# Layer 0 feed-forward: first products over 256 tokens per weight tile, first weights streamed through a ring

## The chip, the core and the metric

The kernel runs on one core of a Trainium2 chip. The time of a run is the device time of one execution in microseconds. The engines are named as the profile names them: PE (TensorE, matmuls; PEld its weight loads), DVE (VectorE), ACT (ScalarE), POOL (GpSimd) and SP (SyncE, which issues most DMAs; its queue is SPq). All data are fp32 unless a row says otherwise.

## What is computed

2048 tokens of 512 features pass two layers, each a cross-attention over a context and a feed-forward (FFN), with a layer norm before each attention and FFN and a residual add behind it. The change touches layer 0's FFN:

```python
inter = xf @ c1_w.T @ c2_w.T                       # rank 16, 1792 columns
blk = inter.reshape(B * T, 56, 32)                 # 56 blocks of 32
idx = jnp.argmax(blk, axis=-1) + jnp.arange(0, 1792, 32)
h = jax.nn.relu(jnp.einsum('bkm,bm->bk', w1[idx], xf))
out = jnp.einsum('bk,bkm->bm', h, w2t[idx])
```

For every token, one of 32 hidden units is chosen in each of 56 blocks. The kernel computes all 1792 hidden values as dense products, keeps the chosen ones (others become zero), and multiplies by the second weights.

## The kernel before

The 2048 tokens are 16 tiles of 128. Layer 0's attention goes over eight pairs of tiles (i = 0 to 7), and behind it comes the FFN, again pair by pair (p = 0 to 7). The instructions of each engine stand in an order that a scheduler of the program's framework makes when the program is built, from priorities and estimated costs. On the chip each engine works its list off in that order and waits for others by semaphores. SP issues its DMAs in order too, with at most eight under way, each waiting for the one eight before it.

A product of matrices is done in Winograd's form of Strassen's scheme: 7 products of quarter matrices in place of 8, in the order `ORDER` = 1, 5, 6, 2, 7, 3, 4 (`winograd`). It needs four sums of quarters of each factor (`four_sums`, L127, on POOL). `keep` copies a partial result on ACT, `put` finishes a quarter of the output.

- **First weights (W1).** During the attention, W1's four quarters are loaded (L610) and their four sums made on POOL. All seven stay in SBUF as tiles of 128 x 2 x 896.
- **Second weights (W2).** They are loaded in pieces during the attention (L516), summed on POOL, stored to HBM (L522), and loaded at the FFN's start (L687, seven loads of 0.9 MB).
- **Preparing a pair.** Layer norm (L104 to L115), transposes on PE (L181) and copies on ACT (L220) give the transposed tokens `xT`. `pz` (L227) and `pzs` (L236) give the rank-16 values, and `key_product` (L279) multiplies them by c2 into `pi`. `first_largest` finds the largest of each block: DVE reduce (L267), DVE compare (L268), a POOL multiply called `e` (L272), DVE reduce (L273). `keep_choice` turns the result on PE (`ptc`, L285), casts it on ACT (L287) and stores it to HBM (L288). `spread_choice` (L673) reads it back onto all partitions, eight DMAs for each part of the hidden columns.
- **Front (first products).** The hidden columns are seven blocks of 128, in two parts, `PARTS` = ((0, 3), (3, 4)). For each part and each of the 7 products, matmuls (L727) of 128 columns, half a pair's tokens. `keep` is L735 (ACT), `put` is L742 (DVE add), L744 (DVE: keeps the value where the spread choice `ch` names this unit, else zero) and L747 (ACT relu). The output is `gT`.
- **Back (second products).** Matmuls (L770) of 256 columns over `gT`, its sums `gs` (POOL), and W2; DVE adds (L778) the result to the tokens `X`.

The loop over pairs puts the back of the pair before between the two parts of a front. The preparation and choice of the next pair are placed there too:

```python
front(xq, gq, ch.pop((p, 0)), 0)
...
back(p - 1, last, between if choosing else lambda i: None)
...
front(xq, gq, ch.pop((p, 1)), 1)
if more:
    ch[p + 1, 1] = spread_choice(p + 1, 1)
    xq = sums(xT)
last = gq + out_sums(gq)
```

Pairs 0 and 1 are prepared and chosen during the attention. The first products accumulate in PSUM tiles `ph`; `pi` is a PSUM tile of four banks of its own. Layer 1 follows, with its products at L901, its weights loaded by SP as tiles of 256 KB.

Of the kernel before, what the change touches and what calls it, by code (L numbers as in the profile page):

```python
# [16 lines left out]
P = 128  # L17
# [3 lines left out]
C = D // P  # L21
# [14 lines left out]
def tile_kernel(  # L36
# [147 lines left out]
    with ExitStack() as l0:  # L184
# [15 lines left out]
        W1 = [w1pool.tile([P, 2, 2 * QW], F32, name=f"w1_{k}", tag=f"w1_{k}") for k in range(4)]  # L200
        w1s = [w1pool.tile([P, 2, 2 * QW], F32, name=f"w1s_{k}", tag=f"w1s_{k}") for k in range(3)]
        W1 += [w1s[0], w1s[1], W1[UNUSED[False]], w1s[2]]


        prepool = l0.enter_context(tc.tile_pool(name="ffnprep", bufs=2, reuse_waits="tile"))
        W2S = [dram.tile([P, HC, 256], F32, name=f"w2s_{k}", tag=f"w2s_{k}") for k in range(4)]

        def prep_steps(p, ps_t):

            xT = prepool.tile([P, C, 2 * P], F32, name=f"xT2_{p}", tag="xT2")  # L210
# [22 lines left out]
            def summed():  # L233
                z = prepool.tile([P, 2 * P], F32, name="z", tag="z", bufs=1)
                pz = ps_t.tile([P, 2 * P], F32, name="pzs", tag="pt")
                nc.tensor.matmul(pz, SUM4.rearrange("p q r -> p (q r)"), held["z"], start=True, stop=True)  # L236
                nc.scalar.copy(z, pz)
                return xT, z
# [5 lines left out]
        def prep(p, ps_t):  # L244
            for step in prep_steps(p, ps_t):
                made = step()
            return made

        def sums(xT):
            q = [xT[:, 2 * k : 2 * k + 2, m * P : (m + 1) * P] for k in range(2) for m in range(2)]  # L250
            s = [prepool.tile([P, 2, P], F32, name=f"xs{k}", tag=f"xs{k}") for k in range(3)]
# [5 lines left out]
        CHOICE = [dram.tile([4 * NBQ, 2 * P], BF16, name=f"choice_{p}", tag=f"choice_{p}") for p in range(NT // 2)]  # L257
# [23 lines left out]
        def keep_choice(p, choices, ps_t):  # L281
# [6 lines left out]
            nc.sync.dma_start(CHOICE[p], ct)  # L288

        def new_choices():  # L290
            return [prepool.tile([P, 4 * NBQ], F32, name="choice", tag="choice", bufs=2) for _ in range(2)]

        with ExitStack() as pa:
# [234 lines left out]
            steps = [prep_steps(p, ps_t) for p in range(2)]  # L528
# [11 lines left out]
            def two_quarters(p, v):  # L540
# [3 lines left out]
                for q in (2 * v, 2 * v + 1):  # L544
                    pi = ps_m.tile([P, 1, D], F32, name="pi0", tag="pm")[:, :, 0:QW]

                    with tc.high_priority(offset=100) if two else ExitStack():
                        key_product(pi[:, 0], made[p][1], q // 4, q % 4)
# [32 lines left out]
            NP = NT // 2  # L581
# [9 lines left out]
            for i in range(NP):  # L591
# [5 lines left out]
                with tc.issue_after(due) if i + 2 < NP else ExitStack():  # L597
                    if store is not None:
                        store()
                    if i:  # L600
# [5 lines left out]
                if 1 <= i < 5:  # L606
                    cols_v = slice(QW * ((i - 1) // 2), QW * ((i - 1) // 2) + QW)
                    for k in (2, 3) if i % 2 else (0, 1):
                        h = 2 * QW * (k // 2)
                        nc.sync.dma_start(  # L610
                            W1[k][:, :, cols_v],
                            w1[:, 2 * (k % 2) : 2 * (k % 2) + 2, h + cols_v.start : h + cols_v.stop],
                        )
# [8 lines left out]
                if i:  # L622
# [5 lines left out]
                    with started_behind(normed):  # L628
                        sum_up()
                        for n in range(*{3: (0, 2), 4: (2, 4), 5: (4, 6), 6: (6, 7), 7: (7, 8)}.get(i, (0, 0))):  # L630
                            w = [t[:, :, QW * (n // 4) : QW * (n // 4) + QW] for t in W1]
                            four_sums(nc.gpsimd, w[4:], *w[:4], False, (n % 4,))
# [17 lines left out]
            xq = sums(made[0][0])  # L650
            xT, choices = made[1][0], choices[1]

        PARTS = ((0, 3), (3, HC - 3))
        with ExitStack() as pb:
            wk = pb.enter_context(tc.tile_pool(name="ffnwork", bufs=2, reuse_waits="tile"))
# [8 lines left out]
            def spread_choice(p, u):  # L666

                c0, n = PARTS[u]
                t = wk.tile([P, 2, n, 2 * P], BF16, name=f"ch{u}_{p}", tag=f"ch{u}", bufs=1)
                d = CHOICE[p].rearrange("(i j b) t -> b i j t", i=2, b=4)  # L670
                for b in range(4):
                    for i in range(2):
                        nc.sync.dma_start(  # L673
                            t[32 * b : 32 * b + 32, i],
                            d[b : b + 1, i, c0 : c0 + n].to_broadcast([32, n, 2 * P]),
# [3 lines left out]
            ch = {(p, u): spread_choice(p, u) for p, u in ((0, 0), (0, 1))}  # L679
# [5 lines left out]
            for i in ORDER:  # L685
# [31 lines left out]
            def front(xq, gq, ch, u):  # L717
# [3 lines left out]
                def bank():  # L721
                    return ps_p.tile([P, n, P], F32, name="ph", tag="pp")

                def mm(i, ps, first):
                    for c in range(n):
                        for d in range(2):
                            nc.tensor.matmul(  # L727
                                ps[:, c, :], W1[LEFT[i]][:, d, (c0 + c) * P : (c0 + c + 1) * P],
                                xq[RIGHT[i]][:, d, :],
                                start=first and c == 0 and d == 0, stop=d == 1, skip_group_check=True,  # L730
                            )

                def keep(k, ps):
                    h = wk.tile([P, n, P], F32, name=f"hk{k}", tag="hk", bufs=3)
# [3 lines left out]
                def put(i, m, ps, kept):  # L738
                    if (i, m) == (1, 1):
                        ps = keep(3, ps)  # L740
                    if kept is not None:
# [3 lines left out]
                        g, ch[:, i, :, m * P : (m + 1) * P], downcol, ps, ALU.is_equal, ALU.mult  # L745
# [3 lines left out]
                winograd(bank, mm, keep, put)  # L749

            def out_sums(gq):
# [5 lines left out]
                for u in range(2):  # L757
                    four_sums(nc.gpsimd, [t[u] for t in s], *(t[u] for t in gq), False)
                return s

            def back(p, gq, between):


                def chunk(q, c):
                    u = int(c >= PARTS[1][0])
                    return q[u][:, c - PARTS[u][0], :]

                def mm(i, ps, first):
# [5 lines left out]
                    between(i)  # L774
# [13 lines left out]
            last = None  # L788
            for p in range(NP):
# [713 lines left out]
```

## Time and profile before

| what | value |
|---|---|
| median of 3 runs | 1797.55 us (1796.15 to 1797.73) |
| the profiled execution, its own time | 1799.84 us |
| its span in the profile | 1798.1 us |
| mean granted TensorE clock | 0.999 |
| layer 0's attention | 0 to 180.65 us of the span |
| layer 0's FFN | 180.65 to about 556 us |

The page gives busy time of each engine, the DMA queues, the chain of work that ended last, and groups of instructions. L numbers are lines of the kernel before. A table by windows gives for each stretch its length, the busy time of PE, PEld, DVE, ACT and POOL with the number of records, the granted clock, the DMA share and GB/s. A line of the chain gives start, length and work; a line of a timeline also gives, in brackets, the idle time before it and what released it.

### The profile page before, as it was taken

What the parts mean: (1) busy time and instruction counts of PE and PEld (TensorE: products, weight loads), DVE (VectorE), ACT (ScalarE), POOL (GpSimd) and SP (SyncE); (2) the same over time, 40 slices, a digit from 0 to 9 for tenths busy, and PEclk for the clock granted to TensorE, in tenths of its full rate; (3) what the DMA queues carried; (4) which work ended last, traced back from release to release, by engine and by line L of the source; (5) the groups of instructions that cost most, each with busy time, mean ns of one, the idle gap of its engine ahead of it and who ended that gap; (6) DMA issues with size and microseconds to landing.
All of it is one profiled execution on the core that took longest, in us unless ns stands there. A gap on an engine that the chain in (4) does not pass through costs nothing.

```text
span 1798.1 us, 29543 instructions
## 1 busy us (share of the span) xinstructions
PE 1773.8 (99%) x11364; PEld 1446.9 (80%) x11364; DVE 968.0 (54%) x1733; ACT 623.0 (35%) x1157; POOL 715.4 (40%) x622
## 2 busy tenths in 40 slices
PE   8999999999999999999999999999999999999999
PEld 4544988988998788888888888888888888888864
DVE  5887565555524454455455444555554555555557
ACT  4654322222112423334234333442343433433311
POOL 1552433443327766764324234332243332322320
PEclk9999999999999999999999999999999999999999
DMA  9632400000014344454444454444445444443513
GB/s 248 195 108 66 166 23 22 22 22 21 13 55 148 130 158 152 141 194 153 147 147 130 143 162 126 132 147 136 135 131 163 137 129 143 149 146 117 182 48 94
DMA packets 169500, 219.31 MB, mean 122 GB/s; under 512 B 19024, under 2 KB 108112, under 8 KB 168720
## 3 DMA queue, kind: packets, MB, share of 16 engines
q1 hardware_dynamic: 155712, 206.91, 37.1%
q10 hardware_dynamic: 13648, 10.50, 2.0%
q8 instruction: 91, 1.49, 0.4%
q14 instruction: 49, 0.40, 0.1%
HBM read 176.74 MB, written 32.21 MB: 116 GB/s over the span
## 4 chain that ended last, share of the span: by engine, by line
PE 88%; POOL 4%; DMA 3%; DVE 2%; ACT 1%; issue 1%; SPq 0%; POOLq 0%; ACTq 0%; DVEq 0%
PE b L901 49%; PE ph L727 10%; PE po L770 10%; PE pv L1130 3%; PE sc L1070 3%; PE pd L1350 3%; PE pq L397 3%; POOL so L127 2%; PE pk L374 2%; PE pr L1048 1%; PE pt L181 1%; PE pi L279 1%; POOL prob L1077 1%; DMA x<-in_x 1%; DMA wos<-wo 1%; PE ptk L1033 1%
## 5 line engine op out<-in xcount | busy, mean ns | idle before, releaser
L1161 DVE TENSOR_TENSOR x<-x,b 128x512 f32<-128x512 f32 x224 | 153.9, 687 | 228.7 <-PE b L901 228.7
L127 POOL TENSOR_TENSOR so<-oT 128x512 f32<-128x512 f32 x64 | 80.1, 1273 | 485.0 <-ACT oT L1137 485.0
L901 PE MATMUL b<-tx,wq 128*128 128x256 f32 x1024 | 237.8, 380 | 3.2 <-DVE qT L994 1.7
L901 PE MATMUL b<-wo,so 128*128 128x256 f32 x1024 | 231.7, 379 | 1.8 <-issue 1.8
L901 PEld LDWEIGHTS b<-tx,wq 128*128 128x128 f32 x1024 | 193.9, 190 | 31.9 <-POOL tx L127 2.5
L901 PEld LDWEIGHTS b<-wo,so 128*128 128x128 f32 x1024 | 194.5, 190 | 28.6 <-issue 2.2
L901 PE MATMUL b<-xt,wq 128*128 128x256 f32 x768 | 183.5, 381 | 0.9 <-DVE kv L965 0.9
L901 PE MATMUL b<-wo,oT 128*128 128x256 f32 x768 | 181.5, 379 | 0.0
L901 PEld LDWEIGHTS b<-xt,wq 128*128 128x128 f32 x768 | 144.4, 190 | 21.2 <-DVE kv L965 1.3
L901 PEld LDWEIGHTS b<-wo,oT 128*128 128x128 f32 x768 | 144.8, 190 | 19.9 <-issue 1.0
L909 ACT COPY keep<-b 128x512 f32<-128x512 f32 x144 | 83.8, 583 | 181.7 <-PE b L901 178.8
L1137 ACT COPY oT<-pv 128x512 f32<-128x512 f32 x64 | 37.4, 584 | 280.6 <-PE pv L1130 270.8
L994 DVE TENSOR_TENSOR qT<-b,keep 128x512 f32<-128x512 f32 x96 | 66.1, 689 | 116.9 <-PE b L901 114.5
L901 PE MATMUL b<-wkv,sc 128*128 128x256 f32 x512 | 117.0, 380 | 0.0
L1082 DVE TENSOR_REDUCE mx<-prob 128x8 f32<-128x512 f32 x64 | 43.9, 686 | 125.0 <-POOL prob L1077 125.0
L901 PEld LDWEIGHTS b<-wkv,sc 128*128 128x128 f32 x512 | 96.6, 190 | 13.8 <-issue 1.0
L272 POOL TENSOR_TENSOR e<-e,down 128x896 f32<-128x896 f32 (+1 forms) x40 | 68.0, 1706 | 93.9 <-DVE e L268 89.8
L997 ACT ACTIVATE qsq<-qT 128x512 f32<-128x512 f32 x128 | 80.3, 627 | 70.5 <-DVE qT L994 58.6
L770 PE MATMUL po<-w,gT 128*128 128x256 f32 x448 | 101.9, 382 | 0.0
L1094 POOL TENSOR_TENSOR prob<-prob,mx 128x512 f32<-128x512 f32 x64 | 66.5, 1060 | 86.0 <-DVE mx L1093 83.6
L770 PEld LDWEIGHTS po<-w,gT 128*128 128x128 f32 x448 | 84.0, 190 | 18.7 <-issue 7.8
L901 PE MATMUL b<-wkv,ct 128*128 128x256 f32 x384 | 93.0, 384 | 2.6 <-DVE mx L1093 2.0
(211 smaller groups left out, 3053.0 us busy)
## 6 DMA issues: line engine op xcount, KB each, us to landing
wq<-in_wq SPq DMA_DIRECT2D x104, 256.0 KB
wo<-in_wo SPq DMA_DIRECT2D x104, 256.0 KB
wq<-wqs SPq DMA_DIRECT2D x96, 256.0 KB
wo<-wos SPq DMA_DIRECT2D x96, 256.0 KB
wkv<-in_wkv SPq DMA_DIRECT2D x52, 256.0 KB
wkv<-wks SPq DMA_DIRECT2D x48, 256.0 KB
wqs<-wq SPq DMA_DIRECT2D x32, 256.0 KB
aT<-tb ACTq DMA_DIRECT2D x256, 32.0 KB
```

What stands on the lines that cost most here:

```text
L127: ins = eng.tensor_tensor(s[k], *pairs[k], op)
L272: nc.gpsimd.tensor_tensor(e3, e3, down[:, None, :].to_broadcast([P, k, BLK]), ALU.mult)
L397: nc.tensor.matmul(pq, xT[:, tt, c, :], WQ[:, c, :], start=c == 0, stop=c == C - 1)
L727: nc.tensor.matmul(ps[:, c, :], W1[LEFT[i]][:, d, (c0 + c) * P : (c0 + c + 1) * P], xq[RIGHT[i]][:, d, :], start=first and c == 0 and d == ...
L770: nc.tensor.matmul(ps, chunk(gq[LEFT[i]], c), W2[RIGHT[i]][:, c, :], start=first and c == 0, stop=c == HC - 1, skip_group_check=True,)
L901: last = nc.tensor.matmul(out[:, h, :], lhs(h, c), rhs(h, c), start=first and h == 0 and c == 0, stop=c == 1, skip_group_check=True,)
L909: keeps.append(nc.scalar.copy(e, ps).ins)
L994: ins = nc.vector.tensor_add(o, ps, kept.rearrange("p j (b t) -> p j b t", t=S))
L997: nc.scalar.activation(qsq[:, 4 * th : 4 * th + 4, 2 * hh : 2 * hh + 2, :], o, AF.Square)
L1070: score = nc.tensor.matmul(sc[b * S : (b + 1) * S, 4 * a + j, :], qT[:, at, j, :], kT[:, bb * S : (bb + 1) * S], start=True, stop=True,)
L1094: ins = nc.gpsimd.tensor_tensor(pr, pr, mx[:, 1, :, None].to_broadcast([P, 8, S]), ALU.mult)
L1161: added.append(nc.vector.tensor_add(xq[:, i, j], xq[:, i, j], ps).ins)
```

## The change

- `PARTS` has four parts, ((0, 2), (2, 2), (4, 2), (6, 1)). A front works on a quad, four tiles (512 tokens), with matmuls of 256 columns. There are four quads (`NQ`).
- W1 is no longer kept in SBUF. Its sums are made in pieces during the attention (`piece_of_w1`, loaded at i = 2 to 5, summed one turn later, stored to HBM four turns after the load), and each front product takes its weight tile from a ring of eight tiles (`load_ring`: 128 x 2 x 256, 256 KB, or half of it for the last part). A tile is loaded when the product that used its slot has been issued; the first eight are loaded at i = 7. Over the kernel 112 tiles are loaded.
- The choice of both pairs of a quad goes to one HBM tensor, and `spread_choice` reads 512 tokens, in four parts of eight DMAs: 128 DMAs in all as before. The second pair's choice is stored at the FFN's start.
- W2's loads are spread over the fronts of the first quad, two with each of its first parts.
- The token sums `xs` are made once for a quad, 128 x 512 each, and the output sums `gs` for each pair in four parts.
- A quad's first back follows the last part of its front; its second back follows the first part of the next quad's front.
- Preparation and choices of the next quad are placed by three tables (FIRST for the first quad, PLAN and LATE for the others).
- The first quad's first part uses the `pi` banks, as one tile of four banks, in place of `ph` tiles.
- The pools of FFN work tiles and of prepared tokens lie on the right side of SBUF; only the pool of `gT` and `gs` stays on the left.

```diff
@@ -197,17 +197,41 @@
             nc.gpsimd.tensor_copy(SUM4[:, q], SUM4[:, 0])
+        PARTS = ((0, 2), (2, 2), (4, 2), (6, 1))
+        NP = NT // 2
+        NQ = NT // 4
+        W1S = [
+            [dram.tile([P, 2, n * P], F32, name=f"w1s_{k}_{u}", tag=f"w1s_{k}_{u}") for u, (_, n) in enumerate(PARTS)]
+            for k in range(4)
+        ]
         W2S = [dram.tile([P, HC, 256], F32, name=f"w2s_{k}", tag=f"w2s_{k}") for k in range(4)]
+        RING = 8
+        ring, rung = [], []
+        W1_ORDER = [(u, i) for _ in range(NQ) for u in range(len(PARTS)) for i in ORDER]
+        def load_ring():
+            if len(ring) == len(W1_ORDER):
+                return
+            u, i = W1_ORDER[len(ring)]
+            (c0, n), k = PARTS[u], LEFT[i]
+            w = w1pool.tile([P, 2, n * P], F32, name=f"w1r_{len(ring)}", tag="w1r", bufs=RING)
+            at = QW * 2 * (k // 2) + c0 * P
+            nc.sync.dma_start(
+                w, w1[:, 2 * (k % 2) : 2 * (k % 2) + 2, at : at + n * P] if k < 4 else W1S[k - 4][u]
+            )
+            ring.append(w)
+        prepool = l0.enter_context(tc.tile_pool(name="ffnprep", bufs=2, side="right", reuse_waits="tile"))
+        def new_tokens(q):
+            return prepool.tile([P, C, 4 * P], F32, name=f"xT2_{q}", tag="xT2")
+        def prep_steps(p, ps_t, quad):
+            xT = quad[:, :, 2 * P * (p % 2) : 2 * P * (p % 2) + 2 * P]
             held = {}
             def norm_tile(m):
...
@@ -525,7 +544,27 @@
-            steps = [prep_steps(p, ps_t) for p in range(2)]
+            def piece_of_w1(u):
+                c0, n = PARTS[u]
+                w = [
+                    w1pool.tile([P, 2, n * P], F32, name=f"w1p_{u}_{k}", tag="w1r", bufs=RING) for k in range(4)
+                ]
+                for k in range(4):
+                    at = 2 * QW * (k // 2) + c0 * P
+                    nc.sync.dma_start(w[k], w1[:, 2 * (k % 2) : 2 * (k % 2) + 2, at : at + n * P])
+                s = prepool.tile([P, 3, 2, n * P], F32, name=f"w1t_{u}", tag="xT2")
+                s = [s[:, 0], s[:, 1], w[UNUSED[False]], s[:, 2]]
+                def store():
+                    for k in range(4):
+                        nc.sync.dma_start(W1S[k][u], s[k])
+                return lambda: four_sums(nc.gpsimd, s, *w, False), store
+            tokens0 = new_tokens(0)
+            steps = [prep_steps(p, ps_t, tokens0) for p in range(2)]
+            pieces = {}
             choices, made, begun, query_added, exped = {}, {}, [], [], []
             def step(p, k):
...
@@ -597,20 +635,19 @@
                 with tc.issue_after(due) if i + 2 < NP else ExitStack():
                     if store is not None:
                         store()
+                    if i - 4 in pieces:
+                        pieces[i - 4][1]()
                     if i:
                         sum_up, store = piece_of_w2(i - 1)
...
+                if 2 <= i < 6:
+                    pieces[i - 2] = piece_of_w1(i - 2)
+                if i == 7:
+                    for _ in range(RING):
+                        load_ring()
...
@@ -627,9 +664,8 @@
                     *scored[i - 1], (_, _, normed) = scores(cn[i - 1], rs1, qT, sq1, kT)
                     with started_behind(normed):
                         sum_up()
-                        for n in range(*{3: (0, 2), 4: (2, 4), 5: (4, 6), 6: (6, 7), 7: (7, 8)}.get(i, (0, 0))):
-                            w = [t[:, :, QW * (n // 4) : QW * (n // 4) + QW] for t in W1]
-                            four_sums(nc.gpsimd, w[4:], *w[:4], False, (n % 4,))
+                        if i - 3 in pieces:
+                            pieces[i - 3][0]()
                 place(i, 1)
                 def between():
...
@@ -663,26 +696,28 @@
-            def spread_choice(p, u):
+            def spread_choice(q, u):
                 c0, n = PARTS[u]
-                t = wk.tile([P, 2, n, 2 * P], BF16, name=f"ch{u}_{p}", tag=f"ch{u}", bufs=1)
-                d = CHOICE[p].rearrange("(i j b) t -> b i j t", i=2, b=4)
+                t = wk.tile([P, 2, n, 4 * P], BF16, name=f"ch{u}_{q}", tag=f"ch{n}", bufs=n)
+                d = CHOICE[q].rearrange("(i j b) t -> b i j t", i=2, b=4)
                 for b in range(4):
                     for i in range(2):
                         nc.sync.dma_start(
                             t[32 * b : 32 * b + 32, i],
-                            d[b : b + 1, i, c0 : c0 + n].to_broadcast([32, n, 2 * P]),
+                            d[b : b + 1, i, c0 : c0 + n].to_broadcast([32, n, 4 * P]),
                         )
                 return t
-            ch = {(p, u): spread_choice(p, u) for p, u in ((0, 0), (0, 1))}
+            keep_choice(1, choices, ps_t)
+            ch = {(0, 0): spread_choice(0, 0)}
             W2 = [
                 None if k == UNUSED[True] else w2pool.tile([P, HC, 256], F32, name=f"w2_{k}", tag=f"w2_{k}")
                 for k in range(8)
             ]
-            for i in ORDER:
+            def load_w2(i):
...
@@ -714,24 +749,24 @@
                 return choose
-            def front(xq, gq, ch, u):
+            def front(xq, gq, ch, u, between, bank):
                 c0, n = PARTS[u]
-                def bank():
-                    return ps_p.tile([P, n, P], F32, name="ph", tag="pp")
                 def mm(i, ps, first):
+                    w = ring[len(rung)]
                     for c in range(n):
                         for d in range(2):
                             nc.tensor.matmul(
-                                ps[:, c, :], W1[LEFT[i]][:, d, (c0 + c) * P : (c0 + c + 1) * P],
-                                xq[RIGHT[i]][:, d, :],
+                                ps[:, c, :], w[:, d, c * P : (c + 1) * P], xq[RIGHT[i]][:, d, :],
                                 start=first and c == 0 and d == 0, stop=d == 1, skip_group_check=True,
                             )
+                    rung.append(i)
+                    load_ring()
+                    between(ORDER.index(i))
...
@@ -742,11 +777,17 @@
+                winograd(lambda: bank(n), mm, keep, put)
+            def halves(gq, m):
+                return [
+                    [g[:, :, t * P : (t + 1) * P] for g in gq[2 * m + i]] for t in range(2) for i in range(2)
+                ]
...
@@ -785,53 +825,122 @@
+            def banks(n):
+                return ps_p.tile([P, n, 2 * P], F32, name="ph", tag="pp")
+            first_banks = iter(range(4))
+            first = ps_i.tile([P, 4, 512], F32, name="pi", tag="pi")
+            def first_bank(n):
+                k = next(first_banks)
+                return first[:, k, 0 : 2 * P * n].rearrange("p (n t) -> p n t", n=n)
+            xT = {0: tokens0}
+            held = {}
+            def start(q):
+                xT[q] = new_tokens(q)
+                held["steps"] = [prep_steps(2 * q + k, ps_t, xT[q]) for k in range(2)]
+            def do(q, k, n):
+                made = held["steps"][k][n]()
+                if n == 4:
+                    held["z"] = made
+            def pick(q, m):
+                if m == 0:
+                    held["choices"] = new_choices()
+                held["choose"] = chosen(held["z"], m, held["choices"][m])
+            def choose(q):
+                held.pop("choose")()
+            def keep(q, k):
+                keep_choice(2 * q + k, held["choices"], ps_t)
+            def spread(q, u):
+                ch[q, u] = spread_choice(q, u)
+            LATE = {
+                ("m0", 0): ((keep, 0), (pick, 0)),
+                ("m0", 1): ((choose,),),
+                ("m0", 2): ((pick, 1),),
+                ("m0", 3): ((choose,),),
+                ("m0", 4): ((keep, 1), (spread, 0)),
+            }
+            FIRST = {
+                (0, 0): ((start,), (do, 0, 0)),
+                (0, 6): ((do, 0, 1),),
+                (1, 3): ((do, 0, 2),),
+                (1, 6): ((do, 0, 3),),
+                (2, 0): ((do, 0, 4),),
+                (2, 3): ((pick, 0),),
+                (2, 6): ((choose,), (do, 1, 0)),
+                (3, 0): ((pick, 1),),
+                (3, 1): ((do, 1, 1),),
+                (3, 4): ((choose,), (do, 1, 2)),
+                (3, 5): ((do, 1, 3),),
+                (3, 6): ((do, 1, 4),),
+            }
+            PLAN = {
+                (0, 3): ((start,), (do, 0, 0)),
+                (0, 6): ((do, 0, 1),),
+                ("m1", 0): ((do, 0, 2), (do, 0, 3)),
+                ("m1", 1): ((do, 0, 4),),
+                ("m1", 2): ((pick, 0),),
+                ("m1", 3): ((choose,),),
+                ("m1", 4): ((pick, 1),),
+                ("m1", 5): ((choose,),),
+                ("m1", 6): ((do, 1, 0),),
+                (1, 3): ((do, 1, 1),),
+                (1, 6): ((do, 1, 2),),
+                (2, 3): ((do, 1, 3),),
+                (2, 6): ((do, 1, 4),),
+            }
+            def placing(q, at):
+                plan = LATE if at == "m0" else FIRST if q == 0 else PLAN
+                def between(k):
+                    if q + 1 < NQ:
+                        for f, *args in plan.get((at, k), ()):
+                            f(q + 1, *args)
+                return between
+            xq, last = sums(tokens0), None
+            for q in range(NQ):
+                gq = new_g()
+                for u in range(len(PARTS)):
+                    if u + 1 < len(PARTS):
+                        spread(q, u + 1)
+                    if q == 0:
+                        for i in ORDER[2 * u : 2 * u + 2]:
+                            load_w2(i)
+                    front(xq, gq, ch.pop((q, u)), u, placing(q, u), first_bank if (q, u) == (0, 0) else banks)
+                    if u == 0 and last is not None:
+                        back(2 * q - 1, last, placing(q, "m1"))
+                left = halves(gq, 0)
+                left = out_sums(left)
+                if q + 1 < NQ:
+                    xq = sums(xT[q + 1])
+                back(2 * q, left, placing(q, "m0"))
+                last = out_sums(halves(gq, 1))
+            back(NP - 1, last, lambda k: None)
```

## Prediction

> **What bounds the kernel now.** I read the page's busy line and its chain first, then the table of windows, then the chain piece by piece, and last the timelines of the queue engines around the start of the layer-0 feed-forward (FFN), at 180.65 us.
>
> ```profile
> PE 1773.8 (99%) x11364; PEld 1446.9 (80%) x11364; DVE 968.0 (54%) x1733; ACT 623.0 (35%) x1157; POOL 715.4 (40%) x622
> PE 88%; POOL 4%; DMA 3%; DVE 2%; ACT 1%; issue 1%; SPq 0%; POOLq 0%; ACTq 0%; DVEq 0%
> ```
>
> TensorE sets the time, and it stands still for only 24 us of the whole span. The windows say where:
>
> ```profile
> 140.00:180.70 40.70, 38.64 (x242) 19.50 (x240) 30.25 (x61) 19.66 (x47) 9.09 (x10) 0.98 0.20 60
> 180.70:216.00 35.30, 35.30 (x310) 34.13 (x308) 16.61 (x31) 14.54 (x30) 12.60 (x13) 0.98 0.58 205
> 216.00:264.00 48.00, 47.91 (x332) 42.85 (x330) 27.94 (x43) 11.32 (x25) 20.46 (x16) 1.00 0.07 21
> 600.00:640.00 40.00, 38.54 (x235) 30.46 (x234) 17.66 (x30) 17.21 (x28) 24.79 (x21) 1.00 0.43 141
> ```
>
> The columns are length, busy PE, PEld, DVE, ACT and POOL, clock, DMA share and GB/s. In the FFN PE has no gap at all, and the waits view names no wait of PE there. So a change in this stage can win only by making PE's own work shorter. It can lose by any wait that it opens. The chain shows what the work costs:
>
> ```profile
> 180.72 10.38 PE ph L727 x84
> ...
> 226.62 12.28 PE po L770 x56
> 239.12 12.51 PE ph L727 x112
> ```
>
> (Columns: start, length, what. The first line comes back below.) A first-product record (128 columns) takes 12.51/112 = 111.7 ns, a second-product record (256 columns) 12.28/56 = 219.3 ns. A matmul leaves two records.
>
> **Part 1, fewer and wider first products.** Before: 8 pairs x 98 matmuls (7 products x 7 column blocks x 2 row blocks) x 2 = 1568 records x 111.7 = 175.1 us. After: 4 quads x 98 x 2 = 784 records of 256 columns x 219.3 = 171.9 us. That is -3.2 us, all on the path. The two rows leave 4 ns per record that does not scale with the columns, and that is all a doubled tile can save. The second products keep their shape: 0. Half the weight loads of the first products go, but they are hidden: PEld is busy 42.85 of 48 us while PE is without gap.
>
> [...]
>
> Moving two pools to the other side of SBUF issues nothing: 0.
>
> **Part 2, W1 through HBM during the attention (to 180 us).** Its quarters are now summed as 128x512 pieces on POOL between the choices of the first pairs, and stored. One such sum takes 1.27 us (the row of the 128x512 `gs`), a piece takes four: 5.1 us. In the instruction order they stand, with the wider token sums, ahead of the POOL step `e` of a choice in the turn around 108 us:
>
> ```profile
> 107.72 1.13 POOL L272 TENSOR_TENSOR e<-e,down 128x448 f32<-128x448 f32 x1
> 109.75 1.13 POOL L272 TENSOR_TENSOR e<-e,down 128x448 f32<-128x448 f32 x1
> ```
>
> By adding durations I get these two done near 114 and 116.5 us, not 108.9 and 110.9. DVE takes its steps in order, so its choice reduction (L273) holds back the `kb` and `kT` work that the scores (L432) need; the chain runs there through DVE already. Bounds: 0 (DVE finds cover) to 5.1 us. I take +3, nearer to what the chain shows. The early loads shrink a little at 0.95 DMA share; PE's idle time there is one wait of 5.5 us for a first weight, so at most 1 us comes back, and I take 0.
>
> **Part 3, the start of the first quad.** This is the heart of the forecast. Before, the first pair needed only its own choice, and its spread was issued from 171.26 us, before the FFN. Now a quad needs both choices, so the second is turned (`ptc`), cast, stored and read back at the FFN's start, with second weights (0.9 MB each) in the queue between. Each of SP's DMAs also waits for the one eight before it.
>
> ```profile
> 171.26 7.44 SPq L673 DMA_DIRECT2D ch<-choice  x16
> 191.75 0.34 SPq L288 DMA_DIRECT2D choice<-choiceT  x1
> 199.25 0.79 SPq L673 DMA_DIRECT2D ch<-choice  x2
> ```
>
> From store to first spread took 7.5 us under load. Landing I bound at 2 to 4 us: a W2 piece of 512 KB issued at 140.9 us was summed from 145.0. Counting t from the FFN's start: store near t+3, first spread between t+6 and t+10.5, eight issues at 0.46 us (7.44/16), landing: the tile `ch` is there between t+12 and t+18. PE covers this by pulling forward products of the second part and token preparation, six products (10.5 us) and some 3 us of transposes in all, and the order shows it running out:
> - The ninth ring tile reuses the slot of the first. It is loaded only when that product is done, and PE wants it one transpose later. Issue 0.5 us and that landing, less the transpose: a stall of about 2.5 us (0 to 4).
> - The token chain transpose, copy (0.57), `pz`, copy (0.37), `pzs`, copy has nothing between on PE in places: about 2.5 us (1 to 4).
> - The first front keeps its products in one tile of four banks, so its product 7 waits for the first put, and the next ones for copies and puts (0.58 + 0.70 + 0.75 us). PE is there at 13.5 + 5 = t+18, when `ch` has landed: about 2 us (0 to 5).
>
> Sum +7 (1 to 13). Sixteen spreads stand before ring tile 10 in SP's queue; it is wanted only near t+23, so this costs 0.
>
> A stall there costs clock as well:
>
> ```profile
> 178.00:180.00 2.00, 1.64 (x9) 0.74 0.55 142
> 180.00:182.00 2.00, 2.00 (x10) 0.50 0.97 306
> ```
>
> After gaps of 0.89, 0.74 and 0.35 us the granted clock fell to 0.50, and the 84 records from 180.72 us took 10.38 us where 84 x 111.7 = 9.38: 1 us lost. I take +1 (0 to 2) for the new gaps. [...]
>
> **Part 4, the ring afterwards.** A 256 KB tile is one product, four matmuls x 2 x 219.3 = 1.75 us, so it needs 150 GB/s in a burst; layer 1 streams 141 GB/s with tiles of that size and no PE wait for them. Eight tiles are 12.3 us of lead behind the one in use. Steady quads: 0. In the first quad eight spreads (3.7 us) and two second weights (1.8 MB, 4.5 us at the 407 GB/s of 182 to 184 us, 9 us at 205) stand ahead of each next group: +1 (0 to 6).
>
> **Part 5, backs and choices.** A back's first product with sums comes one product (14 x 219.3 ns = 3.1 us) after the last front, as the small last part (128x128) is summed; the large parts are summed before: 0. The second quad's preparation and its first pair's choices now fall into the first quad's last two parts, and POOL's `e` steps (2.08 us, two at a time) stand behind three 1.27 us token sums, with DVE's puts of the last part behind the choice: about +2 (0 to 5) before the first back's products with sums. In later quads the second key product waits for the DVE-POOL-DVE chain of the first, 1.08 + 1.09 + 1.08 + 2.08 + 1.08 with handovers about 7.1 us, against two second products, 6.2 us: 0.5 us a time, at most four times, +1 (0 to 6). Layer 1's first weights: PE's idle time at 600 to 640 is 1.5 us, so 0 (-1 to +4).
>
> **Sum.** -3.2 + 3 + 7 + 1 + 1 + 2 + 1 = +11.8 us. The profiled execution took 1799.84 us (span 1798.1), 2.3 above the median of the runs; the difference carries over, so 1797.55 + 11.8, rounded down a little because the terms overlap (one late tile hides another's wait): 1808.5 us. Low ends: all covers hold. High ends: 5 + 13 + 2 + 6 + 5 + 6 + 4 - 3 = +38, never all at once.
>
> **Rivals.**
> 1. The covers hold, faster. Then part 1 counts, and at best 1 us from the early loads, 1.5 at layer 1's start and 2 of PE's idle time at 140 to 180 us: 1789.9 to 1794.4 us. For it: no wait of PE in the FFN before, and an order that pulls work forward. Against: the new dependence on the second choice and the ninth tile's late load, neither of which the old trace has. It decides when all new waits together stay below 3.2 us.
> 2. The ring starves, much slower. If spreads and second weights hold the ring loads past the 12.3 us of lead in every quad, each of four quads loses some 5 to 9 us: +17 to +33 net of part 1, 1815 to 1830. For: one in-order queue with eight in flight. Against: the low DMA share (0.07) that leaves room in the later quads.
> 3. A wash: waits of 0 to 6.5 us in all eat the gain up: 1794.3 to 1800.9.
>
> **How the numbers follow.** A measurement here tells a change from none at about 0.2%, 3.6 us: 1794.0 to 1801.1 is "same". The forecast case (waits that cost 4 to 24 us net) gets 0.62 and rival 2 gets 0.10, both slower: 0.72. Rival 1 gets 0.20, of which 0.17 lies below 1794.0. Rival 3, 0.08, is "same". That gives 0.17, 0.11 and 0.72. The range 1792 to 1824 leaves out the better half of rival 1 and about half of rival 2, and holds the rest.
>
> **What would show it.** Right: records of the first products at 219 ns; PE waits of 2 us or more in the first 25 us of the FFN, on a ring load, on ACT and on DVE puts behind `ch`; the clock below 1.00 there; the FFN longer at its ends, the middle quads without gaps. Wrong: a gap-free first quad, or waits for ring loads (DMA) in all quads, or a first-product record far from 219 ns.

## The result, and the profile after

The changed kernel takes 1856.01 us (median of 6 runs, 1850.97 to 1858.11) against 1797.64 us of the kernel before in the same runs: a ratio of 1.0319, 95% interval 1.0304 to 1.0333. It is 58 us slower, five times the forecast 11, and outside its range. L numbers are now those of the changed kernel: first products L760, second products L810, choice steps L286, L287, L291 (`e`, POOL) and L292, turn of a choice L304.

The page's busy line and its chain (by engine):

```profile
PE 1789.4 (97%) x10580; PEld 1430.4 (77%) x10580; DVE 964.0 (52%) x1733; ACT 624.6 (34%) x1157; POOL 721.5 (39%) x678
PE 84%; POOL 8%; DVE 4%; DMA 2%; issue 1%; ACT 1%; SPq 0%; ACTq 0%; POOLq 0%; DVEq 0%
```

The span grew from 1798.1 to 1854.0 us, by 55.9. PE is busy 15.6 us longer, with 784 records less, and idle for the other 40.3 us (1854.0 - 1789.4 = 64.6, before 24.3). POOL and DVE together hold 12% of the chain, 6% before. Where it happened, by the table of windows (length, busy PE, PEld, DVE, ACT, POOL, clock, DMA share, GB/s):

```profile
100.00:140.00 40.00, 35.35 (x151) 17.64 (x150) 28.45 (x54) 15.87 (x42) 28.26 (x27) 0.87 0.47 153
140.00:180.70 40.70, 39.73 (x227) 20.41 (x227) 29.81 (x58) 19.26 (x44) 13.76 (x17) 1.00 0.36 119
180.70:216.00 35.30, 29.38 (x150) 20.57 (x147) 15.47 (x33) 12.95 (x28) 2.26 (x2) 0.90 0.42 136
216.00:264.00 48.00, 40.89 (x174) 31.73 (x173) 28.64 (x37) 11.94 (x25) 26.76 (x29) 0.89 0.64 209
360.00:408.00 48.00, 40.63 (x187) 33.40 (x186) 23.78 (x33) 6.18 (x13) 24.04 (x28) 0.93 0.26 78
600.00:640.00 40.00, 34.24 (x153) 29.27 (x152) 17.52 (x42) 10.10 (x22) 20.70 (x16) 0.91 0.38 129
```

The five windows in which PE is idle for more than 4 us also have a clock below 1.00; the second (idle 1.0 us) has not. The waits of PE from 100 to 700 us (us in total, times, longest) name the causes:

```profile
PE ptc L304 <- DVE choice L292: 19.0, 4, 5.2
PE pi L298 <- DVE e L287: 6.5, 5, 2.2
PE b L1010 <- issue: 5.8, 1, 5.8
PE psc L451 <- DVE kT L439: 2.3, 1, 2.3
...
PE ph L760 <- DMA w1r<-w1s: 1.8, 2, 1.5
...
PE pi L760 <- DVE gT L779: 1.5, 1, 1.5
```

The largest is the turn of a choice: 5.1 to 5.2 us once in each of quads 0 to 2's first backs, and 3.6 us once more in quad 0. The chain through one of them (start, length, what; the shorter pieces left out) shows what PE waits for:

```profile
364.93 1.07 PE po L810 x4
...
366.07 0.74 POOL gs L127
...
369.09 2.04 POOL e L291
371.13 1.09 POOL gs L127 x2
372.22 1.10 POOL gT L127 x2
373.32 1.37 POOL gs L127 x2
374.69 2.05 POOL e L291
...
380.05 2.09 POOL e L291
...
382.17 1.08 DVE choice L292
383.25 1.01 DVE e L287
...
384.39 2.08 POOL e L291
...
386.50 1.10 DVE choice L292
...
387.64 0.41 PE ptc L304
```

`e` stands behind the output sums (`gs`, `gT`) on POOL; the last step on DVE waits for `e`, the next compare stands behind that step on DVE, and so on through four halves: the choice takes from 364 to 387.6 us. PE meets `ptc` at 382.5, in the middle of the back, and has products behind it that it can't reach.

### The profile page after: what moved, and what is told of

It reads as the page before. It is cut to its first block, busy times and chain, and to the rows that moved or that the text cites. A ratio compares the mean times of both kernels' runs of the same rounds, so it can differ in the third digit from the quotient of the medians.

```text
span 1854.0 us, 28347 instructions
## 1 busy us (share of the span) xinstructions
PE 1789.4 (97%) x10580; PEld 1430.4 (77%) x10580; DVE 964.0 (52%) x1733; ACT 624.6 (34%) x1157; POOL 721.5 (39%) x678
## 4 chain that ended last, share of the span: by engine, by line
PE 84%; POOL 8%; DVE 4%; DMA 2%; issue 1%; ACT 1%; SPq 0%; ACTq 0%; POOLq 0%; DVEq 0%
PE b L1010 49%; PE ph L760 8%; PE po L810 6%; PE pv L1239 3%; PE sc L1179 3%; PE pq L416 3%; PE pk L393 3%; POOL e L291 3%; PE pd L1459 3%; PE pr L1157 1%; POOL so L127 1%; DVE choice L292 1%; PE pt L181 1%; DVE e L287 1%; PE ptk L1142 1%
## 5 line engine op out<-in xcount | busy, mean ns | idle before, releaser
L1010 PE MATMUL b<-tx,wq 128*128 128x256 f32 x1024 | 237.6, 379 | 0.8 <-ACT keep L1018 0.5
L1010 PE MATMUL b<-wo,so 128*128 128x256 f32 x1024 | 231.7, 379 | 1.8 <-issue 1.8
L1010 PEld LDWEIGHTS b<-wo,so 128*128 128x128 f32 x1024 | 194.5, 190 | 28.6 <-issue 2.2
L1010 PEld LDWEIGHTS b<-tx,wq 128*128 128x128 f32 x1024 | 194.1, 190 | 28.9 <-POOL tx L127 1.8
L1010 PE MATMUL b<-xt,wq 128*128 128x256 f32 x768 | 183.5, 381 | 0.9 <-DVE kv L1074 0.9
L1010 PE MATMUL b<-wo,oT 128*128 128x256 f32 x768 | 181.5, 379 | 0.0
L1010 PEld LDWEIGHTS b<-xt,wq 128*128 128x128 f32 x768 | 144.4, 190 | 21.3 <-DVE kv L1074 1.3
L1010 PEld LDWEIGHTS b<-wo,oT 128*128 128x128 f32 x768 | 144.8, 190 | 19.9 <-issue 1.0
L1010 PE MATMUL b<-wkv,sc 128*128 128x256 f32 x512 | 118.2, 382 | 0.0
L1010 PEld LDWEIGHTS b<-wkv,sc 128*128 128x128 f32 x512 | 97.6, 192 | 14.2 <-issue 1.0
L810 PE MATMUL po<-w,gT 128*128 128x256 f32 x448 | 104.1, 388 | 0.0
L1010 PE MATMUL b<-wkv,ct 128*128 128x256 f32 x384 | 94.9, 389 | 8.4 <-issue 5.8
L810 PEld LDWEIGHTS po<-w,gT 128*128 128x128 f32 x448 | 87.1, 196 | 15.8 <-issue 3.3
L291 POOL TENSOR_TENSOR e<-e,down 128x896 f32<-128x896 f32 (+1 forms) x40 | 68.2, 1712 | 78.9 <-DVE e L287 78.5
```

Of the source, the lines that this page charges most:

```text
L291: nc.gpsimd.tensor_tensor(e3, e3, down[:, None, :].to_broadcast([P, k, BLK]), ALU.mult)
L810: nc.tensor.matmul(ps, chunk(gq[LEFT[i]], c), W2[RIGHT[i]][:, c, :], start=first and c == 0, stop=c == HC - 1, skip_group_check=True,)
L1010: last = nc.tensor.matmul(out[:, h, :], lhs(h, c), rhs(h, c), start=first and h == 0 and c == 0, stop=c == 1, skip_group_check=True,)
```

## Experiments

Each kernel is the changed one with the edit shown, and its time is compared with 1856 us; the kernel before ran at 1797.8 to 1798.8 us beside them, and the ratios (with 95% intervals) are to it. Sums below are worked out from these medians.

**1. `e` on DVE.**

```diff
-            nc.gpsimd.tensor_tensor(e3, e3, down[:, None, :]..., ALU.mult)
+            (nc.vector if n == 2 else nc.gpsimd).tensor_tensor(e3, e3, down[:, None, :]..., ALU.mult)
```

> The POOL step `e` of every choice in the feed-forward runs on DVE instead; nothing else is changed. Theory (the choice chain DVE-POOL-DVE is what PE waits for, because `e` queues behind the output sums on POOL and DVE stands behind it in order): the four waits of `ptc` on DVE choice (19.0 us) and the five of `pi` (6.5 us) shrink to 5 us or less in all, the ACT wait of the third part of the first quad (2.0 us) goes, and with the gaps the low clock behind them: 25 to 35 us less, some 1821 to 1831 us. Rival (the chain is too long for the two or three products that cover it, wherever `e` runs): the waits shrink by only the 1 us that one `e` is shorter, 5 to 10 us less, 1846 to 1851 us.

Measured: 1823.76 us, ratio 1.0151 [1.0134, 1.0168], 32 us less. Its waits of PE:

```profile
PE ptc L304 <- DVE choice L292: 2.1, 2, 1.0
PE pi L298 <- DVE e L287: 2.0, 2, 1.2
```

25.5 us of waits became 4.1, and in the quads after the first the granted clock is 1.00 (264 to 552 us). DVE does more than in the changed kernel (988.6 us busy for 964.0) and is no bound. The theory holds: PE was waiting for the way over POOL. From a back's first key product to its last `ptc` record it takes 18.7 us here (349.5 to 368.1 us) and 23.8 us in the changed kernel (363.9 to 387.6). Two things changed at once, and no run separates them: `e` no longer stands behind the output sums, and on DVE its pieces of the chain are 1.00 to 1.14 us long (353.8 to 366.8 us) instead of 2.04 to 2.09.

**2. The turn at the end of the back.**

```diff
-                ("m0", 4): ((keep, 1), (spread, 0)),
+                ("m0", 6): ((keep, 1), (spread, 0)),
```

> The turn of the second pair's choice (`ptc`) stands behind the last product of the back instead of behind its fifth, and its store and spread with it. Theory (PE stands still because an in-order engine meets `ptc` before the choice is done): the three waits of 5.1 us at `ptc` fall to under 1 us, 13 us and some clock, but the spread starts 6 us later for the next quad's first put, which gives 2 to 4 us per quad back: 1840 to 1849 us. Rival (the wait only moves): `ch` is late by as much, 1853 to 1858 us.

Measured: 1836.66 us, 1.0219 [1.0204, 1.0234], 19 us less, more than expected. Of the waits for `ptc`, the one for the first pair's choice in quad 0 is left:

```profile
PE ptc L304 <- DVE choice L292: 4.0, 1, 4.0
```

The three waits of 5.1 us went, and little came back (a new wait of 1.3 us before a second product in the first quad), as the next front has four products (1, 5, 6, 2) before its first put. The kernel before had the turn in this place too: behind the last product of a back, with no wait.

```profile
235.72 3.19 PE L770 MATMUL po<-w,gT 128*128 128x256 f32 x14
238.74 0.38 PE L285 MATMUL ptc<-ident,choice 128*56 128x128 f32 x2
```

So with the choice as slow as before, it is the place of `ptc` in PE's list that makes PE wait. Experiment 1 shortens the chain, this one moves the meeting point.

**3. Order of the second-weight tiles in SBUF.**

```diff
-            W2 = [
-                None if k == UNUSED[True] else w2pool.tile([P, HC, 256], F32, name=f"w2_{k}", tag=f"w2_{k}")
-                for k in range(8)
-            ]
+            W2 = {
+                k: w2pool.tile([P, HC, 256], F32, name=f"w2_{k}", tag=f"w2_{k}")
+                for k in (7, 3, 6, 2, 5, 4, 0)
+            }
```

> The second-weight tiles are laid out in the opposite order in SBUF, so that layer 1's first context tile lies over one that the last back uses first and not over the one it uses last. Theory (the place in SBUF delays that load to the end of the last back): PE's 5.8 us before the first product of layer 1 goes, and some low clock after it: 1848 to 1851 us. Rival (layer 1 starts late for its weights or its norm): no change, 1855 to 1857 us.

Measured: 1846.96 us, 1.0276 [1.0261, 1.0292], 9 us less. The load of layer 1's first context tile, in SP's timelines of the changed kernel and of this one:

```profile
606.20 0.34 SPq L1047 DMA_DIRECT2D ct<-in_cT  x1
```

```profile
588.46 0.34 SPq L1047 DMA_DIRECT2D ct<-in_cT  x1
```

In the changed kernel it is issued when the last back ends (606.2 us), in this one 18 us earlier. PE's wait before L1010 fell from 5.8 to 0.5 us; some 3 us more are clock (0.50 at 612 to 616 us in the changed kernel, 1.00 here).

**4. W1's sums behind the choices of their turn.**

```diff
-                        if i - 3 in pieces:
-                            pieces[i - 3][0]()
...
                 place(i, 2)
+                if i - 3 in pieces:
+                    with tc.issue_after(picked[-1]) if picked else ExitStack():
+                        pieces[i - 3][0]()
```

(`picked` is a list of the `e` instructions.)

> During the attention the four sums of a W1 piece are queued on POOL behind the `e` steps of that turn's choice instead of ahead of them. Theory (part 2 of the forecast): the 2.3 us wait of the scores for kT goes, and the low clock at 117 to 130 us with it (about 4.8 us of 10 are lost there): 5 to 7 us less, 1849 to 1851 us, and the feed-forward starts near 180 us. Rival (the 512-wide token sums or the loads are what delays it): less than 2 us, 1854 to 1857 us.

Measured: 1855.86 us, 1.0325 [1.0310, 1.0341]: nothing gained. The `e` steps were earlier (106.6 and 109.2 us for 110.4 and 112.7), but PE's wait for kT rose to 4.2 us. DVE's timeline says why (the same two lines, of this kernel and then of the changed one):

```profile
113.72 2.25 DVE L108 TENSOR_SCALAR xn<-x,mv,rs 128x512 f32<-128x512 f32 x2
115.89 3.15 DVE L471 SCALAR_TENSOR_TENSOR cn<-cn,rs,fnb 128x512 f32<-128x512 f32 x2
```

```profile
115.77 1.15 DVE L108 TENSOR_SCALAR xn<-x,mv,rs 128x512 f32<-128x512 f32 x2
116.85 1.40 DVE L470 SCALAR_TENSOR_TENSOR cn<-cn,rs,fnb 128x512 f32<-128x512 f32 x2
```

Now POOL's sums (110.2 to 115.7 us) and the `e` pair after them run beside these four DVE steps, which take 5.3 us from the first's start to the last's end instead of 2.5. My theory named the queue; by these rows the neighbourhood costs as much, 2.8 us (5.3 - 2.5). Why the steps take longer there is not shown; no run here separates the causes.

**5. PE's wait filled.**

```diff
+            def fill(q, n):
+                pt = ps_t.tile([P, 256], F32, name="fill", tag="pt")
+                for _ in range(n):
+                    nc.tensor.matmul(pt, ident, W2[3][:, 0, :], start=True, stop=True)
...
-                ("m0", 4): ((keep, 1), (spread, 0)),
+                ("m0", 4): ((fill, 15), (keep, 1), (spread, 0)),
```

> Fifteen matmuls that nobody reads (6.5 us of PE) stand ahead of the turn of the second pair's choice in the first back of quads 0 to 2, in the place of PE's 5.1 us wait; the choice itself takes as long as before. Theory (idle PE lowers its clock, and the low clock costs beside the wait): PE arrives at `ptc` at the same moment, the granted clock stays at 1.00 in the 6 us after, and each of the three places gives 2 to 3 us back although PE does more: 1847 to 1851 us. Rival (what follows the wait is slow for another reason, the wait alone is the cost): 1856 us, or up to 4 us more for the added work.

Measured: 1859.43 us, 1.0335 [1.0314, 1.0356]: no gain. The theory of the clock holds all the same, as the windows of PE alone show (length, busy PE, clock, DMA share, GB/s; first the changed kernel, then this one):

```profile
384.00:388.00 4.00, 0.36 (x2) 0.72 0.00 0
388.00:392.00 4.00, 4.00 (x11) 0.50 0.13 39
392.00:396.00 4.00, 4.00 (x18) 0.93 0.54 141
```

```profile
384.00:388.00 4.00, 4.00 (x21) 1.00 0.02 4
388.00:392.00 4.00, 4.00 (x20) 1.00 0.15 44
392.00:396.00 4.00, 4.00 (x21) 1.00 0.53 142
```

After the wait, the changed kernel needs 6.6 us for 20 second-product records, which are 4.3 us at full clock; here 26 take 5.6 us. So this wait costs 2.3 us more behind it; in the first backs of quads 0 and 2 the 20 records behind waits of 5.2 and 5.1 us took 6.5 and 6.7 us. It is not won here because the filling put both halves of the turn together, six more records behind `ptc`, and in quads 1 and 2 PE came to it 1.5 us later, counted from the start of the back. The trace shows why it came later: the 28 second-product records ahead of the filling took 8.0 us instead of 6.3, behind the wait of 2.2 us for the second key product; the clock was 0.96 at 376 to 380 us and 1.00 from there to 400 us, and by the lengths of the records its mean over the 8.0 us was about 0.79 (6.3/8.0, an estimate). The changed kernel has the same wait of 2.2 us, and the clock stayed at 1.00 behind it (372 to 378 us). The rival's first half is refuted; as a remedy, filling failed.

**6. W1 not summed.**

```diff
-                        nc.sync.dma_start(W1S[k][u], s[k])
+                        nc.sync.dma_start(W1S[k][u], w[k])
 
-                return lambda: four_sums(nc.gpsimd, s, *w, False), store
+                return lambda: None, store
```

> W1's quarters are loaded and stored in pieces as in the changed kernel, but not summed (POOL's 16 sums are left out, the quarters themselves are stored). Theory (the sums delay the attention, by their place ahead of a choice or by running beside DVE): the scores' wait for kT near 120 us falls to the 0.9 us of the kernel before, the low clock at 117 to 130 us goes, and the feed-forward starts 5 to 7 us earlier, 1849 to 1851 us. Rival (the loads and stores of the pieces, or the 512-wide token sums, do it): 1854 to 1857 us.

Measured: 1847.45 us, 1.0267 [1.0250, 1.0285], 8.5 us less. The clock at 100 to 140 us is 1.00 (0.87 in the changed kernel) and the first first-product record (`ph`) starts at 178.8 us instead of 185.2 (180.7 in the kernel before). The 19 us of POOL sums cost 8.5 us on the path; the loads, stores and wider token sums, which stay in, show no cost there.

**7. The first pair's choice for both pairs of the first quad.**

```diff
                 keep_choice(p, choices[p], ps_t)
+                keep_choice(p + 1, choices[p], ps_t)
...
-            keep_choice(1, choices, ps_t)
```

> The first quad uses the first pair's choice for both of its pairs (the second pair's choice is not turned and stored, so it is wrong for 256 tokens); the spread can then be issued during the attention, as in the kernel before. Theory (part 3: the second choice at the start of the feed-forward opens the waits of its first 30 us): of the 5.0 us of waits between 198 and 213 us at least 3.5 go, with the low clock after them: 5 to 8 us less, 1848 to 1851 us. Rival (the token chain and the order of products would make them anyway): 1853 to 1857 us.

Measured: 1843.43 us, 1.0246 [1.0226, 1.0266], 12.6 us less, more than expected. From 180 to 232 us PE waits 0.3 us for DVE (`pi`). From the first product of the feed-forward to the first back it takes 56.9 us instead of 64.1 (7.2 us less), and from there to the second quad's front 34.9 instead of 39.6 (4.6 less). In that back the `ptc` waits fell from 3.6 and 5.2 us to 0.8 and 2.0, while the wait for `e` at the second key product grew from 1.1 to 3.6. A wait of 1.8 us before a first product at 232 us, whose releaser the profile doesn't show, stands where the ring wait of 1.5 us was.

**8. Three mended.** Edits 1 and 3, and the first two W1 pieces loaded and summed one turn earlier (loads at i = 1, 2, 4, 5).

> The choice step `e` on DVE and the opposite order of the second-weight tiles together, and the first two W1 pieces loaded and summed one turn earlier, so that none of that size but the third is summed in the turn around 108 us. Sum of the parts: 1856.0 - 32 - 9 = 1815 us, and 0 to 7 us less if the moved pieces free that turn: 1808 to 1815 us. If the parts shared a wait, it would stay above 1818 us.

Measured: 1824.41 us, 1.0134 [1.0113, 1.0155], 9 us above the sum and above the 1818 us that would speak for a shared wait. The trace shows the place: the scheduler pulled the last two pieces into the turn around 108 us, and PE waited there 3.8 us for kT and 1.8 us for kb. From the first scores to the first product of the feed-forward it takes 155.2 us, 4.7 more than in the changed kernel; the rest of the 9 us was not traced. A step taken out of a crowded place only helps if nothing may move in.

**9. All four taken away.** Edits 1, 3, 6 and 7 together.

> The four suspects taken away together: `e` of the feed-forward on DVE, the second-weight tiles in the opposite order, W1 not summed, and the first pair's choice used for both pairs of the first quad (the last two leave work out). Theory (these four are the whole loss, and the wider first products gain what is left): 1856 less 32, 9, 8.5 and 8 to 13 is 1794 to 1799 us; with some overlap between the first and the last up to 1800 us. Rival (the ring or the new order of fronts and backs costs as well): over 1803 us.

Measured: 1802.74 us, 1.0020 [1.0011, 1.0030], 53 of the 58 us. It lies between the theory (up to 1800 us) and the rival (over 1803): the four are most of the loss and not all of it. The busy line of its profiled execution (1805.76 us):

```profile
PE 1770.8 (98%) x10580; PEld 1417.6 (79%) x10580; DVE 986.0 (55%) x1757; ACT 623.1 (35%) x1157; POOL 663.7 (37%) x638
```

PE is busy 3.0 us less than before the change, near the gain of part 1. It is idle 8.9 us more (1804.0 - 1770.8 = 33.2): some 1.1 us in four of the 48 us windows of the feed-forward, at `ptc` and at products that wait for DVE's adds, and 3.8 us at 216 to 264.

**10. Mended, nothing left out.** Edits 1 and 3; the W1 pieces loaded as in 8, with those of turns 5 and 6 queued behind that turn's `e` steps; and edit 11. **11. The second pair's choice one turn earlier:**

```diff
-                (7, 0): ((two_quarters, 1, 2),),
-                (7, 1): ((choose_begun,),),
+                (6, 2): ((two_quarters, 1, 2),),
+                (7, 0): ((two_quarters, 1, 3),),
+                (7, 1): ((turn_choice, 1),),
...
-            with tc.issue_after(product), tc.issue_after(most):
-                two_quarters(1, 3)
...
-            choose_begun()
...
-            keep_choice(1, choices, ps_t)
```

> All of the computation: `e` on DVE, the second-weight tiles in the opposite order, the W1 pieces summed in turns 2, 3, 5 and 6 of the attention (the later two behind the choices of their turn), and the second pair's choice made one turn earlier, so that it is turned during the last turn. If each suspect can be met this way, 1800 to 1806 us; if the earlier choices delay the attention as the sums did, 1806 to 1816 us.

> The second pair's choice alone is moved one turn earlier in the attention, and its turn into the attention's last turn; nothing is left out. Theory (part 3): as with the known choice, the waits between 198 and 213 us go, 1843 to 1848 us. Rival: the choices' DVE work only moves into the attention and delays it by the same 4 to 8 us, 1851 to 1857 us.

Measured: the mended kernel 1810.42 us, 1.0060 [1.0047, 1.0073], in the range expected if the earlier choices delay the attention; the early choice alone 1849.98 us, 1.0280 [1.0265, 1.0295], 6 us less, between its two expectations and about half of what experiment 7 gained. Both theory and rival are seen in kernel 11: at 200 to 232 us PE has no gap, but from the sixth pair's scores to the first product of the feed-forward it takes 42.3 us instead of 38.2, 1.0 us of it in the softmax wait of the last attention turn (`pa_t` on ACT), which grew from 0.7 to 1.7 us.

**12. Mended, with edit 2 too.**

> As the mended kernel, with the turn of the choice behind the back's last product too. If PE still meets `ptc` early there (2 us of waits were left with `e` on DVE), 1 to 4 us less than the mended kernel; if the spread is then late for the next quad's first put, the same or up to 4 us more.

Measured: 1809.9 us, 1.0061 [1.0048, 1.0074], the same as 10. The 2.1 us at `ptc` went; waits for DVE's adds (L819) before second products and for `xn` rose by 1.9 and 1.0 us. No version here beats the kernel before.

## Why the prediction was wrong, step by step

- **Direction, and the places of the first and second waits: right.** The first quad's gaps came where they were forecast (ring tile, token chain, first put), each 0.3 to 1.5 us where 2 to 2.5 us for each group were forecast. The two `e` steps of the attention came late as forecast, though they were done at 111.5 and 113.8 us and not near 114 and 116.5.
- **Part 5, choices: the failed step.** It held +3 us for the whole feed-forward, 0.5 us a time at the second key product in later quads. It priced the chain of one half against two products, and left out that `ptc` closes four halves and stands in the middle of the back, and that output sums stand on POOL ahead of the first `e` step (3.0 us) and between the first and the second (3.6 us). The waits are 25.5 us in all, 32 us with the clock (experiment 1); the middle quads, forecast without gaps, each lose one wait of 2.2 us and one of 5.1. The chain was named; its length was not added up for the whole choice, and `ptc`, where PE meets its end, was not named for the backs. Even at the second key product its own figures, 7.1 against 6.2 us, give 0.9 us and not 0.5; the waits there measured 1.1 to 2.2 us.
- **The clock: mis-sized.** Forecast +1 us. PE's busy time is 18.6 us above that of experiment 9, which does almost the same work; experiment 5 shows 2.3 us for one place. I had the row (0.50 after three short gaps) and priced it for one spot, not for every new wait. The five gaps of 3.6 to 5.8 us here come to some 12 of the 18.6 us at 2.3 us each (an estimate from experiment 5). The clock was low behind shorter gaps too: at 120 us, behind gaps of 0.6, 0.9 and 2.3 us, it was 0.50, and PE's records from the scores to the end of `pq` took 14.2 us, 9.6 in the kernel before.
- **Layer 1's start: wrong.** I gave 0 to the other side of SBUF because it issues nothing. The new layout puts a context tile over the last second-weight tile in use: 9 us (experiment 3).
- **Part 2: right in kind, low in price.** Forecast +3, measured 8.5 (experiment 6): 2.3 us of wait at 120 us and half clock until nearly 130 us. That four DVE steps took 5.3 us instead of 2.5 beside POOL's sums and `e` steps (experiment 4) was not foreseen.
- **Part 3: about right.** Forecast +7 and clock +1; experiment 7 gives 12.6, of which 7.2 us lie before the first back and 4.6 us in it, in choice waits that I had in part 5.
- **Part 4: right.** Ring waits are 1.8 us, all in the first quad (forecast +1); rival 2, the starving ring, is refuted, and the later quads have none.
- **Part 1: right to within a few us.** -3.2 forecast, -3.0 in PE's busy time of experiment 9. A first-product record is 12.09/56 = 215.9 ns in the chain, not 219.3. With that figure the same sum would have read -5.8 us, so the close agreement is in part luck; why the row behind 219.3 was longer is not shown.
- **Rival 1** needed all covers to hold; four did not.

The singles add up to 32 + 9 + 8.5 + 12.6 = 62 us, together they give 53: the first quad's choice waits are in both the first and the last. What stays open is the last 4 us of experiment 9; its small waits were listed, not removed one by one.

## What to carry to other kernels

Where an in-order engine meets the end of a chain across two others, add up the whole chain with all that is queued between its steps, and compare it with the work up to the meeting point, not with the stage. Price a new gap of TensorE twice, for itself and for the slow clock that may follow it; here the clock was 0.50 behind a gap of 5.1 us, and behind a gap of 2.2 us it fell in one run and not in another. A change of SBUF layout can have a price even if it issues nothing (9 us in experiment 3): look at which tile the next stage's first load has to wait for.

## What the runs showed of the hardware

In the changed kernel, after a gap of 5.1 us (382.5 to 387.6 us), the granted clock was 0.50 until 5 us after PE resumed. After gaps of 0.6, 0.9 and 2.3 us within 6 us it was 0.50 from 120 to nearly 130 us; DMA moved 245 to 398 GB/s in most of that time, and whether this plays a part is not shown. After the same gap of 2.2 us it stayed at 1.00 in the changed kernel and fell in experiment 5 (0.96 at 376 to 380 us, and 28 records in 8.0 us instead of 6.3 before that), so the length of a gap alone did not decide. DVE's `xn` and `cn` steps (128x512) took 0.5 and 0.7 us each with little beside them (changed kernel, 116.4 to 118.3 us) and 1.1 and 1.6 us beside POOL's sums and `e` steps (experiment 4, 113.7 to 119.0 us), while of those the later two sums took 1.46 instead of 1.27 us and the two `e` steps 1.42 instead of 1.13 us each. DVE's `kb` step (L396, L397) took 0.74 us in both kernels, in experiment 4 beside a sum. Why is not shown.
